# A graph-network stack on one core: the row of f_j by one small transpose and four SBUF-to-SBUF transfers, LayerNorm and mask in place, five groups

## The chip, the cores and the metric

The kernel runs on one core of one Trainium2 chip, as one program. The metric is the device time of that core in microseconds, as the median of several runs. The kernel before takes 2701.74 us (three runs, 2699.85 to 2704.03).

## The reference

128 graphs of 128 nodes with 256 features each go through four layers, all in float32. Each layer is followed by a residual sum and a LayerNorm. The first is a gated graph network of three steps, the other three are graph attention with different weights:

```python
# layer 0, three times:
m = jnp.einsum('bnd,de->bne', h, weight[i])
aggr = jnp.einsum('bst,bsd->btd', A, m)          # A = (adj != 0)
h = _gru_cell(aggr, h, w_ih, w_hh, b_ih, b_hh)
# layers 1 to 3:
Wh = jnp.einsum('bnf,of->bno', h, W)
f_i, f_j = Wh @ a1, Wh @ a2
e = f_i[:, :, None] + f_j[:, None, :]
e = jnp.where(e > 0, e, ALPHA * e)
e = jnp.where(adj == 0, NEG_INF, e)
h_prime = jnp.einsum('bij,bjo->bio', jax.nn.softmax(e, axis=2), Wh)
# after each layer
x = _layernorm(x + layer(x, adj, ...))
```

What the change touches is the second term of `e`: for every graph the vector f_j, one value per node, has to stand as a row in all 128 partitions, because partition i holds row i of the scores.

## The kernel before, in words

The graphs are worked in 32 groups of G = 4. For a group, `gru` (L477) loads x and the adjacency, turns the adjacency into a float mask (L489), transposes x (L369), and runs three steps. A step aggregates the states over the graph (L504) and forms the gates by `strassen` (L434): seven block products for each of two calls, matmuls of 128x128 by 128x256 (L451), accumulated in PSUM banks of the tag `gate`. DVE adds the parts (L456), ACT takes them out (L512, L516, L519), tanh comes from ACT (L530, L559), the mixing of old and new state from DVE and POOL (L546 to L569). After each step the state is transposed back (L585). After the third, x is loaded again into a buffer `y` (L575), the state is added (L588), and the mask is turned into a bias of 0 or a very large negative number (L576).

Then `gat` (L601) runs the three attention layers of the group. The scores' two vectors f_j (h = 1) and f_i (h = 0) come from eight DVE multiplications with a running sum, one for each graph and vector (L611), which land as columns of a small tile `f`. The row of f_j is made on TensorE: four transposes (L620) of a column that is broadcast to 128 columns, one for each graph, into one PSUM bank. DVE adds the bias and takes the row's maximum (L625), ACT applies the leaky slope (L629) and the exponential (L646), TensorE transposes the weights (L653), multiplies them with the features (L669) and with the layer's matrix (L680), DVE adds the residual (L686), and `layernorm` (L375) follows: mean (L391), squares on ACT (L394), 1/sqrt on POOL (L397, L401), scale and shift on ACT (L407). The group's result is stored (L693).

Nothing of this is issued in the order of the source. Each operation is put into `Plan` with the engines that may run it, a duration for each, what it reads and writes, and a priority. `Plan.order` simulates the engines with these durations and emits the instructions in the order in which they started there; on the chip every engine works through its own list in that order. An operation starts only when its operands are due and when slots for its buffers are free:

```python
LATENCY = {"PE": 250, "ACT": 220, "DVE": 200, "POOL": 250, "SP": 4000}
```

is added between a producer and a consumer on another engine (a transfer counts 4000 ns from its issue, and `lag` on top), and a consumer on TensorE gets 500 ns more. Buffers come in tags with a fixed number of slots, among them `k4` (4 KB a partition), `k2` (2 KB), `bank` (3 PSUM banks), `gate` (5 PSUM banks), `v` (small columns), and `gru`, which has no memory and only limits how many groups are in their gated steps at once; `own` keeps a part of the slots for the oldest group. The priority comes from `stage` (L696): group g has the first number g throughout, and the last four groups (LAST = 4) go step by step together. SyncE (SP) issues all bulk transfers, in order. An operation that names `port=BOTH` is not placed beside another[...]; by default only POOL's operations hold it.

## Time and profile before

| | |
|---|---|
| time, median of three runs | 2701.74 us |
| span of the profiled execution | 2698.8 us |
| busy TensorE / DVE / ACT / POOL | 98 / 75 / 65 / 22% |
| DMA moved in all | 65.39 MB, 24 GB/s over the span |

A matmul in float32 of L451 shows up as two records, one of weights and data each, a transpose as one. Records of TensorE overlap[...]. What an instruction takes of the engine is read from start to start. "PEld" is the loading of weights, which runs beside matmuls.

### The profile page before, as it was taken

How to read it: one execution, taken by the hardware profiler on the slowest of the kernel's cores; microseconds unless marked ns; L12 is line 12 of the kernel's file. 1: busy time of each engine (PE TensorE's matmuls, PEld its weight loads, DVE VectorE, ACT ScalarE, POOL GpSimd, SP SyncE). 2: the span in 40 equal slices, each digit the busy share in tenths (PEclk: the TensorE clock that was granted, in tenths of full speed). 3: DMA queues.
4: the chain of work that ended last, by engine and by line, in shares of the span. 5: the costliest groups of instructions: out<-in, count | busy, mean ns of one | idle time of the engine just before them, and what ended most of it. 6: DMA issues, size and time to landing. Idle time of an engine off the chain costs nothing.

```text
span 2698.8 us, 42460 instructions
## 1 busy us (share of the span) xinstructions
PE 2655.6 (98%) x14536; PEld 2366.9 (88%) x14536; DVE 2019.6 (75%) x6195; ACT 1758.2 (65%) x4633; POOL 603.7 (22%) x749
## 2 busy tenths in 40 slices
PE   8999999999999999999999999999999999999997
PEld 7888889898888888888888888988988988888875
DVE  4676777787777787778777777877778776786796
ACT  4565667666667576666666676666666676765478
POOL 1123222222121221222221221211222211322111
PEclk9999999999999999999999999999999999999999
DMA  3100000000000000001010000000000100000000
GB/s 106 32 13 28 28 13 24 28 29 20 16 21 20 28 28 28 28 1 36 21 36 13 20 24 21 28 28 20 17 28 21 36 21 1 24 9 22 19 1 32
DMA packets 70105, 65.39 MB, mean 24 GB/s; under 512 B 2688, under 2 KB 68224, under 8 KB 69888
## 3 DMA queue, kind: packets, MB, share of 16 engines
q1 hardware_dynamic: 69456, 62.66, 7.7%
q8 instruction: 114, 1.87, 0.3%
q14 instruction: 103, 0.84, 0.1%
q10 hardware_dynamic: 432, 0.01, 0.0%
HBM read 45.89 MB, written 16.78 MB: 23 GB/s over the span
## 4 chain that ended last, share of the span: by engine, by line
PE 90%; DVE 6%; ACT 2%; issue 1%; DMA 0%; POOL 0%; POOLq 0%; ACTq 0%; SPq 0%; DVEq 0%
PE gate L451 61%; PE bank L680 10%; PE bank L504 6%; PE bank L669 6%; PE bank L585 3%; PE bank L620 1%; PE bank L653 1%; DVE fx L611 1%; PE bank L369 1%; PE bank L338 1%; DVE k L686 1%; ACT k L407 1%; DVE k L456 1%; DVE k L289 1%; ACT k L394 0%
## 5 line engine op out<-in xcount | busy, mean ns | idle before, releaser
L451 PE MATMUL gate<-k,whs 128*128 128x256 f32 x4032 | 1201.6, 380 | 3.0 <-DVE k L456 1.4
L451 PE MATMUL gate<-k,wcs 128*128 128x256 f32 x4032 | 1199.2, 379 | 0.0
L451 PEld LDWEIGHTS gate<-k,wcs 128*128 128x128 f32 x4032 | 766.1, 190 | 104.0
L451 PEld LDWEIGHTS gate<-k,whs 128*128 128x128 f32 x4032 | 728.5, 190 | 85.3 <-DVE k L456 2.7
L456 DVE TENSOR_TENSOR k<-gate,k 128x512 f32<-128x512 f32 x576 | 390.4, 686 | 242.3 <-PE gate L451 200.2
L287 ACT COPY k<-bank 128x512 f32<-128x512 f32 (+1 forms) x456 | 262.2, 583 | 207.4 <-PE bank L669 60.9
L680 PE MATMUL bank<-gwT,k 128*128 128x256 f32 x1536 | 350.4, 380 | 3.3 <-ACT k L287 1.5
L680 PEld LDWEIGHTS bank<-gwT,k 128*128 128x128 f32 x1536 | 289.7, 190 | 46.0 <-DVE k L289 4.3
L611 DVE SCALAR_TENSOR_TENSOR fx<-k,wa 128x256 f32<-128x256 f32 x768 | 290.3, 436 | 40.3 <-ACT k L407 38.2
L421 POOL TENSOR_TENSOR k<-k,k 128x256 f32<-128x256 f32 x288 | 236.0, 838 | 372.8 <-DVE k L569 103.6
L394 ACT ACTIVATE k<-k,v 128x256 f32<-128x256 f32 x384 | 190.2, 497 | 185.6 <-DVE v L391 185.1
L407 ACT ACTIVATE k<-k,v,v 128x256 f32<-128x256 f32 x512 | 263.6, 591 | 55.9 <-DVE v L403 53.9
L530 ACT ACTIVATE k<-k,brz 128x512 f32<-128x512 f32 (+1 forms) x384 | 226.9, 620 | 93.2 <-DVE k L456 93.1
L686 DVE SCALAR_TENSOR_TENSOR k<-bank,v,k 128x256 f32<-128x256 f32 x384 | 169.9, 480 | 147.0 <-PE bank L680 145.8
L512 ACT COPY k<-gate 128x512 f32<-128x512 f32 x288 | 164.6, 579 | 127.9 <-PE gate L451 127.0
L564 POOL TENSOR_TENSOR k<-k,k 128x512 f32<-128x512 f32 x82 | 108.5, 1324 | 418.0 <-ACT k L559 418.0
L669 PEld LDWEIGHTS bank<-k,k 128*128 128x128 f32 x1536 | 187.1, 193 | 14.6 <-ACT k L287 5.4
L669 PE MATMUL bank<-k,k 128*128 128x128 f32 x1536 | 189.8, 277 | 8.0 <-DVE k L289 4.0
L289 DVE COPY k<-bank 128x512 f32<-128x512 f32 x228 | 154.3, 684 | 56.2 <-PE bank L504 18.3
L559 ACT ACTIVATE k<-k,bi 128x512 f32<-128x512 f32 x192 | 136.8, 720 | 76.3 <-DVE k L556 59.2
L397 POOL TENSOR_SCALAR v<-v 128x4 f32<-128x4 f32 x96 | 21.1, 220 | 739.3 <-ACT k L394 733.3
L421 POOL TENSOR_TENSOR k<-k 128x256 f32<-128x256 f32 x117 | 100.2, 858 | 340.4 <-DVE k L569 118.2
(78 smaller groups left out, 3166.8 us busy)
## 6 DMA issues: line engine op xcount, KB each, us to landing
xs<-in_x_dram SPq DMA_DIRECT2D x32, 512.0 KB, 3.9
k<-in_x_dram SPq DMA_DIRECT2D x32, 512.0 KB, 3.9
out_dram<-k SPq DMA_DIRECT2D x32, 512.0 KB, 2.9
adj<-in_adj_dram SPq DMA_DIRECT2D x32, 256.0 KB, 2.8
k<-in_gnn_wT_dram SPq DMA_DIRECT2D x3, 256.0 KB, 4.8
k<-in_w_ihT_dram SPq DMA_DIRECT2D x2, 384.0 KB, 5.7
k<-in_w_hhT_dram SPq DMA_DIRECT2D x2, 384.0 KB, 5.7
k<-in_gat_w_dram SPq DMA_DIRECT2D x3, 256.0 KB, 5.1
```

What stands on the lines that cost most here:

```text
L287: nc.scalar.copy(dst, src)
L289: nc.vector.tensor_copy(dst, src)
L394: plan.op({"ACT": 490}, lambda e, b=b: nc.scalar.activation(T(dst)[:, b, :], T(y)[:, b, :], AF.Square, bias=T(mean)[:, b:b + 1], accum_out ...
L407: plan.op({"ACT": 500}, lambda e, b=b: nc.scalar.activation(T(dst)[:, b, :], T(y)[:, b, :], AF.Identity, bias=T(shift)[:, b:b + 1], scale= ...
L421: nc.vector if e == "DVE" else nc.gpsimd).tensor_tensor(T(t)[:, j, :], a(), b(), ALU.subtract),
L451: nc.tensor.matmul(T(dst)[:, j * H:(j + 1) * H], T(w)[:, m, gt, :], moving(m, ms)[1](), start=first and n == 0, stop=n == len(todo) - 1, s ...
L456: plan.op({"DVE": 630}, lambda e: nc.vector.tensor_add(T(o)[:, :, j * H:(j + 1) * H], T(b_).rearrange("p (g n) -> p g n", g=2), T(part).re ...
L530: nc.scalar.activation(T(o)[:, gt, n0:n1], src(), AF.Tanh, bias=brz[:, gt * KC + c:gt * KC + c + 1], scale=0.5)
L611: plan.op({"DVE": 345}, lambda e, b=b, h=h, l=l, f=f, fx=fx, xc=xc: nc.vector.scalar_tensor_tensor(T(fx), T(xc)[:, b, :], 1.0, T(wa)[:, l, ...
L669: nc.tensor.matmul(T(b_)[:, b * P:(b + 1) * P], T(xc)[:, b, c * P:(c + 1) * P], T(pT)[:, b, :], start=True, stop=True)
L680: nc.tensor.matmul(T(b_)[:, (b - b0) * D:(b - b0 + 1) * D], T(aT[k])[:, b * P:(b + 1) * P], T(gwT)[:, l, k, :], start=(k == 0), stop=(k == ...
L686: nc.vector.scalar_tensor_tensor(T(y)[:, b, :], T(b_)[:, (b - b0) * D:(b - b0 + 1) * D], T(rden)[:, b:b + 1], T(xc)[:, b, :], op0=ALU.mult ...
```

## The change

The row of f_j takes another way, for all groups but the last four. One transpose turns the 128x4 columns of f_j into a tile of 4x128 in PSUM; ACT or DVE copies it to SBUF (`row`); then SyncE issues four transfers, one for each graph, which read one row of 512 bytes and write it to all 128 partitions of the score tile `e_`. The bias is added to it in place (L625 of before). The purpose is to take work off TensorE and to hold the PSUM bank more briefly.

The other edits change buffers and order. LayerNorm writes into its own input, with the squares into a scratch tile `jx`. The adjacency is loaded into the mask's own buffer, so that the tag `adj` goes. The second load of x starts after the first tanh of the last step and not after the first aggregation. There may be five groups in their gated steps and six masks, `fx` has one slot, the reserves of `own` are other ones, and the attention of group g has the priority g + 1.5.

```diff
-    pools = {"gru": 4, "xs": 2, "adj": 2, "am": 5, "k2": 26, "k4": 19, "fx": 2, "f": 3, "mv": 4, "st": 6, "v": 16,
+    pools = {"gru": 5, "xs": 2, "am": 6, "k2": 26, "k4": 19, "fx": 1, "jx": 1, "f": 3, "row": 3, "mv": 4, "st": 6, "v": 16,
              "gate": 5, "bank": 3}
-    own = ({"k2": 8, "k4": 5, "gate": 2, "v": 5, "fx": 0, "st": 0}, {"k2": 4, "k4": 2, "v": 5, "fx": 0, "st": 0})
+    own = ({"k2": 6, "k4": 5, "v": 5, "fx": 0, "jx": 0, "st": 0}, {"k2": 6, "k4": 3, "v": 5, "fx": 0, "jx": 0, "st": 0})
...
-                plan.op({"ACT": 490}, lambda e, b=b: nc.scalar.activation(
-                    T(dst)[:, b, :], T(y)[:, b, :], AF.Square, bias=T(mean)[:, b:b + 1], accum_out=T(ss)[:, b:b + 1]),
-                    reads=[(y, b), mean], writes=[(dst, b), (ss, b)], prio=prio)
+                jx = Buf("jx", D)
+                plan.op({"ACT": 490}, lambda e, b=b, jx=jx: nc.scalar.activation(
+                    T(jx), T(y)[:, b, :], AF.Square, bias=T(mean)[:, b:b + 1], accum_out=T(ss)[:, b:b + 1]),
+                    reads=[(y, b), mean], writes=[jx, (ss, b)], prio=prio)
...
-                T(dst)[:, b, :], T(y)[:, b, :], AF.Identity, bias=T(shift)[:, b:b + 1], scale=T(rstd)[:, b:b + 1]),
-                reads=[(y, b), shift, rstd], writes=[(dst, b)], prio=prio)
+                T(y)[:, b, :], T(y)[:, b, :], AF.Identity, bias=T(shift)[:, b:b + 1], scale=T(rstd)[:, b:b + 1]),
+                reads=[(y, b), shift, rstd], writes=[(y, b)], prio=prio)
...
-                plan.op({"SP": 60}, lambda e: nc.sync.dma_start(T(y), x_g), reads=[agg[0]], writes=[y], prio=prio)
+                plan.op({"SP": 60}, lambda e: nc.sync.dma_start(T(y), x_g), reads=[(nn[0], 5)], writes=[y], prio=prio)
...
             b_ = bank()
-
-            def fn(e, b_=b_, f=f):
+            if g < NG - LAST:
+                row = Buf("row", P)
+                plan.op({"PE": 150}, lambda e, b_=b_, f=f: nc.tensor.transpose(T(b_)[0:G, 0:P], T(f)[:, :, 1], ident),
+                        reads=[(f, 2 * b + 1) for b in range(G)], writes=[b_], prio=prio)
+                plan.op({"ACT": 250, "DVE": 200}, lambda e, b_=b_, row=row: copy(e, T(row)[0:G, :], T(b_)[0:G, 0:P]),
+                        reads=[b_], writes=[row], prio=prio)
                 for b in range(G):
-                    nc.tensor.transpose(T(b_)[:, b * P:(b + 1) * P],
-                                        T(f)[:, b, 1:2].to_broadcast([P, P]), ident)
-            plan.op({"PE": 440}, fn, reads=[(f, 2 * b + 1) for b in range(G)], writes=[b_], prio=prio)
+                    plan.op({"SP": 330}, lambda e, b=b, row=row, e_=e_: nc.sync.dma_start(
+                        T(e_)[:, b, :], T(row)[b:b + 1, :].unsqueeze(1).to_broadcast([1, P, P])),
+                        reads=[row], writes=[(e_, b)], prio=prio, lag=1500)
+                rows, keys, port = (lambda b, e_=e_: T(e_)[:, b, :]), lambda b: [], BOTH
+            else:
+                def fn(e, b_=b_, f=f):
+                    for b in range(G):
+                        nc.tensor.transpose(T(b_)[:, b * P:(b + 1) * P],
+                                            T(f)[:, b, 1:2].to_broadcast([P, P]), ident)
+                plan.op({"PE": 440}, fn, reads=[(f, 2 * b + 1) for b in range(G)], writes=[b_], prio=prio)
+                rows, keys, port = (lambda b, b_=b_: T(b_)[:, b * P:(b + 1) * P]), lambda b, b_=b_: [b_], ("POOL",)
 
             for b in range(G):
-                plan.op({"DVE": 215}, lambda e, b_=b_, b=b, e_=e_, top=top: nc.vector.tensor_tensor_reduce(
-                    T(e_)[:, b, :], T(b_)[:, b * P:(b + 1) * P], T(no)[:, b, :], 1.0, 3 * FAR, ALU.add, ALU.max,
-                    T(top)[:, b:b + 1]), reads=[b_, no], writes=[(e_, b), (top, b)], prio=prio)
+                plan.op({"DVE": 215}, lambda e, rows=rows, b=b, e_=e_, top=top: nc.vector.tensor_tensor_reduce(
+                    T(e_)[:, b, :], rows(b), T(no)[:, b, :], 1.0, 3 * FAR, ALU.add, ALU.max,
+                    T(top)[:, b:b + 1]), reads=keys(b) + [no, (e_, b)], writes=[(e_, b), (top, b)], prio=prio, port=port)
...
-            xn = Buf("k4", G, D)
-            layernorm(y, total, xn, prio)
-            xc = xn
+            layernorm(y, total, prio)
+            xc = y
...
-        return g if g < tail else tail + n, 2 * g + (n >= STEPS)
+        return g + 1.5 * (n >= STEPS) if g < tail else tail + n, 2 * g + (n >= STEPS)
```

More of the change, by code (lines that the diff above doesn't have):

```diff
@@ L221, in adj_resnorm_kernel @@
     psum = ctx.enter_context(tc.tile_pool(name="psum", bufs=1, space=bass.MemoryType.PSUM))
-    pools = {"gru": 4, "xs": 2, "adj": 2, "am": 5, "k2": 26, "k4": 19, "fx": 2, "f": 3, "mv": 4, "st": 6, "v": 16,
+    pools = {"gru": 5, "xs": 2, "am": 6, "k2": 26, "k4": 19, "fx": 1, "jx": 1, "f": 3, "row": 3, "mv": 4, "st": 6, "v": 16,
              "gate": 5, "bank": 3}
-    own = ({"k2": 8, "k4": 5, "gate": 2, "v": 5, "fx": 0, "st": 0}, {"k2": 4, "k4": 2, "v": 5, "fx": 0, "st": 0})
-    floats = {"gru": 0, "k4": 1024, "xs": 1024, "fx": 256, "f": 8, "mv": 8, "st": 6, "v": 4}
+    own = ({"k2": 6, "k4": 5, "v": 5, "fx": 0, "jx": 0, "st": 0}, {"k2": 6, "k4": 3, "v": 5, "fx": 0, "jx": 0, "st": 0})
+    floats = {"row": 128, "gru": 0, "k4": 1024, "xs": 1024, "fx": 256, "jx": 256, "f": 8, "mv": 8, "st": 6, "v": 4}
     tags = {t: (n, floats.get(t, 512)) for t, n in pools.items()}
@@ L230, in adj_resnorm_kernel @@
     plan = Plan({t: n for t, (n, _) in tags.items()}, own)
-    slots = {t: [(psum if t in ("gate", "bank") else work).tile([P, w], I32 if t == "adj" else F32, name=f"{t}{i}")
+    slots = {t: [(psum if t in ("gate", "bank") else work).tile([P, w], F32, name=f"{t}{i}")
                  for i in range(n)] for t, (n, w) in tags.items() if w}
@@ L373, in transposed, with layernorm @@
         return res
-    def layernorm(y, total, dst, prio):
+    def layernorm(y, total, prio):
         rstd, ve, shift = Buf("v", G), Buf("v", G), Buf("v", G)
@@ L477, in gru @@
     def gru(g, stage):
-        xs, adj_i, am = Buf("xs", G, D), Buf("adj", G, P), Buf("am", G, P)
+        xs, am = Buf("xs", G, D), Buf("am", G, P)
         prio = stage(g, 0)
@@ L483, in gru @@
         plan.op({"SP": 450}, lambda e: nc.sync.dma_start(T(xs), x_g), writes=[xs], prio=prio)
-        plan.op({"SP": 60}, lambda e: nc.sync.dma_start(T(adj_i), adj[g * G:(g + 1) * G].rearrange("b s t -> s b t")),
-                writes=[adj_i], prio=prio)
+        plan.op({"SP": 60}, lambda e: nc.sync.dma_start(T(am).bitcast(I32), adj[g * G:(g + 1) * G].rearrange("b s t -> s b t")),
+                writes=[am], prio=prio)
         if g == 0:
@@ L488, in gru @@
             hidden_weights(prio)
-        plan.op({"DVE": 417}, lambda e: nc.vector.tensor_scalar(T(am), T(adj_i), 0, None, op0=ALU.not_equal),
-                reads=[adj_i], writes=[am, turn], prio=prio, port=BOTH)
+        plan.op({"DVE": 417}, lambda e: nc.vector.tensor_scalar(T(am), T(am).bitcast(I32), 0, None, op0=ALU.not_equal),
+                reads=[am], writes=[am, turn], prio=prio, port=BOTH)
         hT = transposed(xs, lambda b, c: T(xs)[:, b, c * P:(c + 1) * P], prio)
@@ L596, in gru @@
                 h, hT = h2, hT2
-        x1 = Buf("k4", G, D)
-        layernorm(y, None, x1, prio)
-        return x1, am
+        layernorm(y, None, prio)
+        return y, am
     def gat(g, xc, no, stage):
```

## The prediction

> **What bounds the kernel now.** I read the page first (busy shares, then the chain that ended last), then the busy time by stage, then the order in time around one set of the transposes that go.

> The page's busy shares and its chain that ended last:

> ```profile
> PE 2655.6 (98%) x14536; PEld 2366.9 (88%) x14536; DVE 2019.6 (75%) x6195; ACT 1758.2 (65%) x4633; POOL 603.7 (22%) x749
> ...
> PE 90%; DVE 6%; ACT 2%; issue 1%; DMA 0%; POOL 0%; POOLq 0%; ACTq 0%; SPq 0%; DVEq 0%
> PE gate L451 61%; PE bank L680 10%; PE bank L504 6%; PE bank L669 6%; PE bank L585 3%; PE bank L620 1%; PE bank L653 1%; DVE fx L611 1%; PE bank L369 1%; PE bank L338 1%; DVE k L686 1%; ACT k L407 1%; DVE k L456 1%; DVE k L289 1%; ACT k L394 0%
> ```

> TensorE is busy 98% of the span and 90% of the chain is TensorE itself: almost never a wait, nearly always the instruction before. L620, the set of four transposes that the change takes out, is named in it with 1%.

> Busy time of each engine by stage (columns: stretch, length, PE, PEld, DVE, ACT, POOL, granted clock, DMA share and GB/s):

> ```profile
> 0.00:200.00 200.00, 188.28 (x956) 162.41 (x957) 125.37 (x298) 105.59 (x246) 36.24 (x45) 0.99 0.17 51
> 200.00:400.00 200.00, 198.47 (x1088) 177.24 (x1087) 142.18 (x421) 125.77 (x325) 47.22 (x58) 1.00 0.07 22
> 400.00:2400.00 2000.00, 1995.12 (x11029) 1789.82 (x11029) 1531.94 (x4697) 1328.16 (x3513) 471.74 (x584) 1.00 0.08 23
> 2400.00:2600.00 200.00, 199.70 (x1054) 176.61 (x1052) 145.14 (x375) 117.13 (x282) 32.03 (x38) 1.00 0.05 14
> 2600.00:2698.80 98.80, 74.03 (x414) 60.86 (x414) 74.94 (x408) 81.55 (x271) 16.51 (x26) 0.95 0.07 22
> ```

> The average hides two kernels. From 400 to 2400 us TensorE idles 4.9 us in 2000; DVE idles 23% and ACT 34% there. All of TensorE's idle time is 2698.8 - 2655.6 = 43.2 us, of which 11.7 lie in the first 200 us and 24.8 in the last 99. So in the middle a microsecond less of matmul is a microsecond less of span, as long as the others keep feeding TensorE; the end is another matter.

> One set in the order of time of TensorE (start, duration, then the instruction):

> ```profile
> 1003.80 0.59 PE L451 MATMUL gate<-k,wcs 128*128 128x256 f32 x2
> 1004.23 0.60 PE L620 MATMUL bank<-ident,f 128*128 128x128 f32 x4
> 1004.67 0.60 PE L451 MATMUL gate<-k,whs 128*128 128x256 f32 x2
> ```

> Durations overlap; the starts count. The next matmul starts 1004.67 - 1004.23 = 0.44 us after the set does, so one transpose takes 0.11 us of TensorE, though its record says more (next fence). A pair of L451 records takes 0.43 us.

> [...] No transfer of the kernel before reads so few partitions, so the trace is silent; this is the main risk. [...] L546, both inputs in SBUF, averages 743 ns; L456, one input in PSUM, 686.

> **The change part by part.** The rows that price it, from the groups of instructions and the DMA issues (busy, mean ns; for DMA us to landing):

> ```profile
> L620 PE MATMUL bank<-ident,f 128*128 128x128 f32 x384 | 59.1, 274 | 2.5 <-DVE fx L611 1.3 <-DVE k L686 1.0
> L625 DVE CUSTOM_DVE_ANT_0 k<-bank,am 128x128 f32<-128x128 f32 x384 | 88.3, 285 | 12.2 <-PE bank L620 11.8
> L519 ACT COPY k<-gate 128x256 f32<-128x256 f32 x288 | 105.2, 366 | 0.0
> ```

> ```profile
> k<-in_x_dram SPq DMA_DIRECT2D x32, 512.0 KB, 3.9
> adj<-in_adj_dram SPq DMA_DIRECT2D x32, 256.0 KB, 2.8
> ```

> *Removed.* 28 of the 32 groups times 3 layers are 84 sets of four transposes, 84 x 4 x 0.11 = 37.0 us of TensorE; the last four groups keep theirs.

> *Added on TensorE.* 84 small transposes. The identity is still the moving operand with 128 columns, only the stationary side shrinks to four, so I take 0.11 us; the bounds are 0.03 (if four columns cost a quarter) and 0.22 (if its neighbours' weight loads, 190 ns each, were not hidden). 84 x 0.11 = 9.2 us. Net: 37.0 - 9.2 = **27.7 us less**, all of it between 100 and 2600 us, on the path. With the bounds: 34.4 to 18.5.

> *Added copies.* 84 copies of 4x128 from PSUM. The nearest row is L519, 366 ns for twice the columns; I take 0.3 us, 84 x 0.3 = 25 us, on ACT or DVE, hidden in ACT's 34% or DVE's 23% of idle time.

> *Added transfers.* 84 x 4 = 336 of 64 KB each (a row of 512 B, written to 128 partitions), 0.37 us each for SyncE to issue: 124 us in all on a queue with some 130 issues in it, hidden. Landing: 256 KB take 2.8 us and 512 KB 3.9, so 1.1 us per 256 KB and 1.7 fixed; 64 KB come to 2.0 us. The four are issued within 1.1 us, so the last row is there 3.1 us after SyncE starts, or 5 if an x load lies ahead of it. [...] The plan in the code allows 4 x 0.33 + 1.5 + 4.0 = 6.8 us for the last row. I take something at or below 6.8, then DVE finds its rows there.

> *The added wait.* It is L625's, for the transfer. Behind it on DVE, which runs in order, stand the additions L456 that empty the gate banks, and TensorE waits for these. Within the 6.8 us nothing waits, since the order puts other work ahead of L625.

> *DVE.* The reduce reads two SBUF operands in place of PSUM and SBUF. By [...]L546 against L456 at most 8% longer: 336 x 0.02 = 8 us, in DVE's idle time. Its four no longer hold one of the three PSUM banks: a small gain for TensorE, which I don't count.

> *Latency of a layer.* Copy, issue and landing add 4 to 7 us to a layer. Two x loads of L575 start at 988.36 and 1074.23, so a group takes 86 us and a layer's share is 28; the fifth group and the later place of the attention (1.5 later in priority) keep more ready work beside it. In the middle I cost it at nothing: TensorE has other groups' gates to do.

> *In place.* LayerNorm into y, squares into a scratch tile, the mask where its integers landed: the same instructions, cost 0; k4 buffers come free earlier. One slot of fx or jx alters the order alone, since one engine writes it. The y load now starts after the first tanh of the last step; between are three DVE operations of 0.69 us and the transposes of 0.44, 2.5 us, against 3.9 to land, so L588 comes up to 1.4 us later, 32 x 1.4 = 45 us of one of three banks, off TensorE's path.

> *Start and end.* The last four groups keep the old form, and the 24.8 us idle in the last 99 us stay. I leave the first 200 us as they are too.

> Sum: 2701.7 - 27.7 = **2674.0 us**.

> **Rivals.** A, the forecast: transfers within their time, TensorE still dense, 2674; with the bounds 2667 to 2683.

> B, denser too: freed buffers, the shorter hold of a bank and the fifth group also remove the middle's 6.7 us of idle and half of the first 200 us' 11.7: 27.7 + 6.7 + 5.9 = 40.3, 2661. For it: waits for banks are what TensorE's few gaps consist of. Against: there is little left to gain.

> C, gain eaten: the long round trip costs TensorE some 0.25 us in each of the 84 layers, 21 us, so 2695. For it: a static order fits one set of latencies. Against: DVE idles 28 x 0.23 = 6.5 us a layer, which absorbs such slips.

> D, slower: [...] For it: [...]DVE's order. Against: L625 has lower priority than the next group's gates, so often stands later than its rows' due time, and the four rows are wanted one after another.

> **How the numbers follow.** A 0.58, B 0.10, C 0.12, D 0.20. The time is A's. For eight in ten the range takes A with its bounds, B to 2656 and C with a little of D's mild end, to 2714; most of D stays out. The limits of 0.2% are 2696.3 and 2707.1: A, B and half of C are below, 0.74; between lies 0.08 (the rest of C and the edge of D); above 0.18.

> **What would show it.** Right: TensorE busy about 28 us lower with its share still 98%, the middle's idle time still near 5 us in 2000, the row transfers landing in 2 to 6 us, the groups showing 84 small transposes with 0.11 us between their start and the next, and no wait of DVE for a DMA above some tens of us. Wrong: waits of L625 for the transfers of hundreds of us, TensorE then idling before L451 with L456 as the releaser[...]. A tail with more than 30 us idle would show that the order got worse at the end.

## The result, and the profile after

The changed kernel takes 3001.11 us (median of four runs, 2997.41 to 3005.13) beside 2702.81 us of the kernel before: 1.1106 times as long, 95% interval 1.1086 to 1.1125. It is 298 us slower where 27.7 us less were forecast.

The page of the changed kernel, busy shares and the chain that ended last. Its lines are shifted: L452 is L451 of before, L457 is L456, L638 is the reduce (L625 of before), L620 the small transpose, and L625 is now the transfer of a row.

```profile
PE 2755.8 (92%) x14284; PEld 2400.4 (80%) x14284; DVE 2091.3 (70%) x6220; ACT 1770.2 (59%) x4600; POOL 706.0 (24%) x841
...
PE 53%; DMA 22%; DVE 15%; ACT 5%; issue 3%; SPq 2%; POOL 1%; POOLq 0%; ACTq 0%; DVEq 0%
PE gate L452 31%; DMA k<-row 21%; PE bank L693 8%; PE bank L682 5%; PE bank L505 4%; DVE k L457 3%; DVE fx L611 2%; DVE k L289 2%; PE bank L586 2%; SPq L625 2%; ACT k L659 2%; DVE k L547 1%; PE bank L666 1%; POOL v L402 1%; DVE st L382 1%
```

TensorE fell from 90 to 53% of the chain, and the transfers of the rows, absent before, are 21% of it. TensorE is busy longer in all than before, though it has 252 instructions less.

The stages (stretch, length, PE, PEld, DVE, ACT, POOL, granted clock, DMA share and GB/s):

```profile
200.00:400.00 200.00, 175.47 (x930) 154.15 (x929) 130.22 (x395) 113.60 (x296) 38.03 (x47) 0.95 0.28 27
400.00:2400.00 2000.00, 1849.24 (x9581) 1614.29 (x9580) 1420.96 (x4181) 1180.49 (x3075) 516.88 (x607) 0.95 0.30 29
2900.00:2998.80 98.80, 74.11 (x424) 63.07 (x422) 72.42 (x391) 83.57 (x270) 16.19 (x26) 0.90 0.07 22
```

The loss lies in the middle: TensorE has 9581 records in these 2000 us where it had 11029, idles 150.8 us where it idled 4.9, and its granted clock is 0.95 where it was 1.00. The last 99 us are as before (74.1 us busy, 74.0 before). The DMA engines are busy 30% of the time where they were 8, for 29 GB/s in place of 23: a lot of time for few bytes.

From the groups of instructions and the DMA issues, the rows that answer to those of before:

```profile
L620 PE MATMUL bank<-ident,f 128*4 128x128 f32 x84 | 23.0, 274 | 4.3 <-DVE fx L611 4.0 <-ACT k L513 0.2
L638 DVE CUSTOM_DVE_ANT_0 k<-k,am 128x128 f32<-128x128 f32 x336 | 114.1, 349 | 307.3 <-DMA k<-row 307.3
```

```profile
k<-row SPq DMA_DIRECT2D x336, 64.0 KB, 8.5
xs<-in_x_dram SPq DMA_DIRECT2D x32, 512.0 KB, 4.1
```

The 84 small transposes are there. A row of 64 KB takes 8.5 us to land, twice as long as x with 512 KB. DVE stands 307 us before L638 for it.

How that reaches TensorE is seen in one place: first SyncE, which issues the transfers, then DVE, then TensorE, each in order of time:

```profile
1256.34 16.83 SPq L625 DMA_DIRECT2D k<-row  x8
```

```profile
1263.62 0.29 DVE L638 CUSTOM_DVE_ANT_0 k<-k,am 128x128 f32<-128x128 f32 x1 [1.66 <-DMA k<-row]
...
1266.17 0.29 DVE L638 CUSTOM_DVE_ANT_0 k<-k,am 128x128 f32<-128x128 f32 x1 [1.90 <-DMA k<-row]
1266.39 0.08 DVE L638 DVE_READ_ACCUMULATOR2_ANT v<- 128x1 f32 x1
1268.22 0.29 DVE L638 CUSTOM_DVE_ANT_0 k<-k,am 128x128 f32<-128x128 f32 x1 [1.75 <-DMA k<-row]
1268.44 0.08 DVE L638 DVE_READ_ACCUMULATOR2_ANT v<- 128x1 f32 x1
1268.44 0.69 DVE L457 TENSOR_TENSOR k<-gate,k 128x512 f32<-128x512 f32 x1
```

```profile
1265.82 0.59 PE L452 MATMUL gate<-k,wcs 128*128 128x256 f32 x2
1271.60 1.22 PE L452 MATMUL gate<-k,whs 128*128 128x256 f32 x2 [5.18 <-DVE k L457]
1272.61 1.06 PE L452 MATMUL gate<-k,wcs 128*128 128x256 f32 x2
```

The line of SyncE spans the issues of two layers, four transfers each, with a pause of 8.8 us between them. The four of the first layer start at 1256.34 to 1258.14 and land at 1260.91, 1263.60, 1266.15 and 1268.20. DVE finds the first row there and waits 1.7 to 1.9 us before each of the other three. So it goes in 54 of the 84 layers; in 19 DVE does not wait at all. The gate additions L457 stand behind; TensorE uses up what it has and waits 5.18 us for them. Then its matmuls start 1.01 us apart where they started 0.43 apart. The windows of 4 us over this place say why (the column before the last two is the granted clock):

```profile
1262.00:1266.00 4.00, 4.00 (x22) 3.54 (x21) 0.65 (x4) 1.00 (x3) 0.00 (x0) 1.00 0.72 25
1266.00:1270.00 4.00, 0.41 (x2) 0.01 (x1) 2.08 (x10) 1.32 (x4) 0.00 (x0) 0.97 0.28 11
1270.00:1274.00 4.00, 2.40 (x7) 1.94 (x8) 3.61 (x11) 3.51 (x12) 0.80 (x1) 0.50 0.68 25
1274.00:1278.00 4.00, 4.00 (x19) 3.75 (x18) 3.44 (x6) 0.77 (x2) 1.50 (x2) 0.68 0.72 25
```

The granted clock falls to 0.50 in the idle stretch, 3.3 us after its start, and stays there for 6.8 us, the last 5.0 of them after TensorE has begun again. The 300.0 us between the two spans add up: idle 43.2 before and 243.0 after, so 199.8 more; busy 2655.6 before and 2755.8 after, so 100.2 more, although about 27.7 us of work went. That leaves 127.9 us of longer work, most of it the lower clock: the trace has the clock at 0.50 for 259.9 us, TensorE is busy in 190.1 of them, and at half the rate 95 are lost; before it was 3. So the clock costs about 92 us, an estimate. The other 36 stay open. TensorE stops more often, with 210 busy stretches where it had 59, and the last record of each has no next one to overlap with; that may be it, but no run shows it alone.

### The profile page after: what moved, and what is told of

Same layout as the page of the kernel before. It is cut to its first block, busy times and chain, and to the rows that moved or that the text cites. A ratio compares the mean times of both kernels' runs of the same rounds, so it can differ in the third digit from the quotient of the medians.

```text
span 2998.8 us, 42377 instructions
## 1 busy us (share of the span) xinstructions
PE 2755.8 (92%) x14284; PEld 2400.4 (80%) x14284; DVE 2091.3 (70%) x6220; ACT 1770.2 (59%) x4600; POOL 706.0 (24%) x841
## 4 chain that ended last, share of the span: by engine, by line
PE 53%; DMA 22%; DVE 15%; ACT 5%; issue 3%; SPq 2%; POOL 1%; POOLq 0%; ACTq 0%; DVEq 0%
PE gate L452 31%; DMA k<-row 21%; PE bank L693 8%; PE bank L682 5%; PE bank L505 4%; DVE k L457 3%; DVE fx L611 2%; DVE k L289 2%; PE bank L586 2%; SPq L625 2%; ACT k L659 2%; DVE k L547 1%; PE bank L666 1%; POOL v L402 1%; DVE st L382 1%
## 5 line engine op out<-in xcount | busy, mean ns | idle before, releaser
L452 PE MATMUL gate<-k,whs 128*128 128x256 f32 x4032 | 1242.8, 391 | 124.5 <-DVE k L457 106.9
L452 PE MATMUL gate<-k,wcs 128*128 128x256 f32 x4032 | 1225.0, 386 | 0.0
L452 PEld LDWEIGHTS gate<-k,whs 128*128 128x128 f32 x4032 | 743.3, 195 | 238.6 <-DVE k L457 125.5
L452 PEld LDWEIGHTS gate<-k,wcs 128*128 128x128 f32 x4032 | 785.2, 195 | 113.1
L457 DVE TENSOR_TENSOR k<-gate,k 128x512 f32<-128x512 f32 x576 | 390.7, 686 | 287.0 <-PE gate L452 205.9
L565 POOL TENSOR_TENSOR k<-k,k 128x512 f32<-128x512 f32 x134 | 171.7, 1282 | 1306.7 <-ACT k L560 1303.7
L642 ACT ACTIVATE k<-k,f 128x128 f32<-128x128 f32 x384 | 148.3, 400 | 375.9 <-DVE v L638 375.8
L611 DVE SCALAR_TENSOR_TENSOR fx<-k,wa 128x256 f32<-128x256 f32 x768 | 343.7, 448 | 14.0 <-ACT k L408 3.6
L638 DVE CUSTOM_DVE_ANT_0 k<-k,am 128x128 f32<-128x128 f32 x336 | 114.1, 349 | 307.3 <-DMA k<-row 307.3
L422 POOL TENSOR_TENSOR k<-k,k 128x256 f32<-128x256 f32 x344 | 273.5, 809 | 230.0 <-ACT k L287 65.3
L531 ACT ACTIVATE k<-k,brz 128x256 f32<-128x256 f32 (+1 forms) x384 | 233.8, 623 | 75.6 <-DVE k L457 75.6
L395 ACT ACTIVATE jx<-k,v 128x256 f32<-128x256 f32 x384 | 193.8, 505 | 114.2 <-DVE v L391 108.1
L289 DVE COPY k<-bank 128x512 f32<-128x512 f32 x293 | 198.0, 685 | 87.3 <-PE bank L666 30.2
L659 ACT ACTIVATE k<-k,v 128x128 f32<-128x128 f32 x384 | 149.4, 390 | 43.0 <-DVE v L655 40.6
## 6 DMA issues: line engine op xcount, KB each, us to landing
xs<-in_x_dram SPq DMA_DIRECT2D x32, 512.0 KB, 4.1
k<-in_x_dram SPq DMA_DIRECT2D x32, 512.0 KB, 4.2
out_dram<-k SPq DMA_DIRECT2D x32, 512.0 KB, 3.2
am<-in_adj_dram SPq DMA_DIRECT2D x32, 256.0 KB, 2.8
k<-in_gnn_wT_dram SPq DMA_DIRECT2D x3, 256.0 KB, 5.6
```

The costliest lines, as they stand in the source:

```text
L289: nc.vector.tensor_copy(dst, src)
L395: plan.op({"ACT": 490}, lambda e, b=b, jx=jx: nc.scalar.activation(T(jx), T(y)[:, b, :], AF.Square, bias=T(mean)[:, b:b + 1], accum_out=T( ...
L422: nc.vector if e == "DVE" else nc.gpsimd).tensor_tensor(T(t)[:, j, :], a(), b(), ALU.subtract),
L452: nc.tensor.matmul(T(dst)[:, j * H:(j + 1) * H], T(w)[:, m, gt, :], moving(m, ms)[1](), start=first and n == 0, stop=n == len(todo) - 1, s ...
L457: plan.op({"DVE": 630}, lambda e: nc.vector.tensor_add(T(o)[:, :, j * H:(j + 1) * H], T(b_).rearrange("p (g n) -> p g n", g=2), T(part).re ...
L531: nc.scalar.activation(T(o)[:, gt, n0:n1], src(), AF.Tanh, bias=brz[:, gt * KC + c:gt * KC + c + 1], scale=0.5)
```

## Experiments: is it where the rows lie?

The theory, T: the transfers are slow because of where their rows lie, each in one partition and the four in partitions 0 to 3; DVE stands before them and starves TensorE. The rivals: S, small transfers are slow whatever they read; O, the new order and the buffers cost the time; L, five groups cannot hide a longer layer.

**Reading 128 partitions.** The same transfers in the same order, from another place:

```diff
-  nc.tensor.transpose(T(b_)[0:G, 0:P], T(f)[:, :, 1], ident)
+  nc.tensor.transpose(T(b_)[:, 0:P], T(f)[:, 0, 1:2].to_broadcast([P, P]), ident)
...
-  T(e_)[:, b, :], T(row)[b:b + 1, :].unsqueeze(1).to_broadcast([1, P, P])
+  T(e_)[:, b, :], T(row)
```

> The changed kernel with the same 336 transfers of 64 KB in 128 packets of 512 bytes, in the same order, but each reads 128 partitions in place of one: the small transpose makes the row of the first graph in all 128 partitions, and each transfer copies it partition by partition. It leaves out the rows of f_j of the other three graphs. Theory T: the packets take 30 to 60 ns in place of about 220, landing falls from 8.5 to between 2 and 3 us, the wait of DVE for the transfers from 307 to below 30 us, and the time is 2665 to 2690 us. Rival S (small transfers, their issue or their number are slow in themselves): landing stays above 6 us and the time above 2900. Rival O: landing falls but the time stays above 2800.

It took 2672.24 us, 0.9892 times the kernel before (0.9877 to 0.9907). Packets of 512 bytes, those of the rows and of the adjacency together, took 27 ns in the median, where those of the changed kernel took 220. The page's busy shares, the middle stage and the landing:

```profile
PE 2630.0 (98%) x14284; PEld 2341.2 (88%) x14284; DVE 2083.2 (78%) x6220; ACT 1747.9 (65%) x4600; POOL 698.7 (26%) x841
```

```profile
400.00:2400.00 2000.00, 1998.83 (x10954) 1788.14 (x10954) 1605.98 (x4750) 1330.06 (x3520) 573.61 (x685) 1.00 0.11 33
```

```profile
k<-row SPq DMA_DIRECT2D x336, 64.0 KB, 1.9
```

Same number, size and order of transfers; landing 1.9 in place of 8.5 us, no wait of DVE for rows in the waits, the clock at 1.00 in the middle, 329 us gone. S and O fall as the main cause.

**Four rows 36 partitions apart.** A kernel in which DVE first spreads the columns of f_j to 4x32, so that the transpose gives 32 copies of each row, was run with two sources for the transfers. In the first of them each transfer reads one partition, and the four are 0, 36, 72 and 108:

```diff
-  T(row)[b:b + 1, :].unsqueeze(1).to_broadcast([1, P, P])
+  T(row)[36 * b:36 * b + 1, :].unsqueeze(1).to_broadcast([1, P, P])
```

> As the run with the spread source, but each transfer reads one partition again: partition 36 b for graph b[...]. If the DMA engines take the transfers strictly one after another[...]: landing near 4.6, 7.3, 9.8 and 11.9 us after the first issue, 2950 to 3060 us. If the engines overlap transfers, the four go in parallel: all landed within some 6 us, below 2800 us.

Counted from the first issue of a layer, the medians over its 84 layers and those of the changed kernel are:

| row | changed kernel, us | 36 apart, us | 128 partitions, us |
|---|---|---|---|
| 1 | 4.59 | 4.01 | 1.81 |
| 2 | 7.28 | 4.85 | 2.46 |
| 3 | 9.83 | 5.34 | 3.09 |
| 4 | 11.88 | 6.90 | 3.73 |

The rows land as in the second answer of the expectation, though the last at 6.9 us and not at 6: with the rows 36 partitions apart they follow one another by 0.5 to 1.6 us. In the changed kernel, from partitions 0 to 3, they do so by 2.05 to 2.7 us: 65,536 bytes in 2.43 us on average, 27.0 GB/s. What makes the one set of partitions slower than the other is not shown. The time was still 2953.43 us (1.0932, 1.091 to 1.0953), as in the first answer, and most of that is not the rows: the next run has the same order.

**32 partitions a transfer**, all of f_j computed:

```diff
+  nc.vector.tensor_copy(T(fw).rearrange("p (b r) -> p b r", b=G), T(f)[:, :, 1:2].to_broadcast([P, G, 32]))
-  nc.tensor.transpose(T(b_)[0:G, 0:P], T(f)[:, :, 1], ident)
+  nc.tensor.transpose(T(b_)[:, 0:P], T(fw), ident)
...
-  T(row)[b:b + 1, :].unsqueeze(1).to_broadcast([1, P, P])
+  T(row)[32 * b:32 * b + 32, :].unsqueeze(1).to_broadcast([32, G, P])
```

> The changed kernel, computing all it should, with the rows' source spread: DVE copies each column of f_j 32 times into a tile of 128x128 (one more instruction for a group's layer, two row slots in place of three for space), the one transpose then yields 32 copies of each graph's row, and a transfer reads 32 partitions four times each in place of one 128 times. [...] packets of 30 to 60 ns, landing 1.8 to 3 us, DVE's wait for rows below 30 us, 2662 to 2690 us, so faster than both kernels. If reading a partition more than once is what is slow[...], landing stays above 4 us and the time above 2750.

The rows landed within 2.09 to 4.03 us, as expected. The time, 2919.22 us (1.0802, 1.0786 to 1.0818), is 34 us below the run with rows 36 partitions apart but 229 us above the expected range. TensorE waits elsewhere (waits of TensorE, total, times, longest):

```profile
PE bank L669 <- ACT k L662: 59.3, 16, 5.9
PE bank L623 <- DVE fw L620: 39.8, 11, 9.3
```

The additional copy and the softmax come late in this order. I had taken two row slots in place of three for space. With three, and one slot for the spread tile:

> The run with the spread source of 32 partitions again (2919 us, rows landed by 4.0 us, TensorE waiting up to 9 us for the spread copy), with three row slots as in the changed kernel and one unreserved slot for the spread tile, in place of two and two. If the two row slots made that order bad (a slot is held until the planned landing, and one is kept for the oldest group): 2665 to 2700 us. If the spread source or the additional DVE copy is what costs: above 2800 us.

2743.11 us (1.0156, 1.0139 to 1.0173), between the two answers. The 2919 us lie 244 above the best version found below (2675). Of these, 176 go with the two slot counts, which were not tried apart; the other 68 stay open, since the copy and its one slot change the order too.

## Experiments: latency, order and the other edits

**The measured due times given to the plan**, the transfers as slow as ever:

```diff
-  reads=[row], writes=[(e_, b)], prio=prio, lag=1500)
+  reads=[row], writes=[(e_, b)], prio=prio, lag=(1500, 3300, 5500, 7300)[b])
```

> The changed kernel, with one edit: the plan's lag of the four row transfers is 1.5, 3.3, 5.5 and 7.3 us in place of 1.5 for all, so that the order expects the rows at 5.8, 8.0, 10.5 and 12.6 us after the first issue; the trace shows 4.6, 7.3, 9.8 and 11.9. The transfers themselves stay as slow. Theory T in its weak form (what costs is that DVE meets the wait, not the latency): DVE's wait below 60 us, the clock back at 0.99 or more, 2670 to 2720 us. Rival L (five groups cannot hide a longer layer): 2850 us or more with little wait of DVE for transfers, and TensorE idle for lack of ready work.

2735.33 us (1.0127, 1.0111 to 1.0142): 266 us of the loss are gone without a faster transfer. The waits of this kernel:

```profile
DVE k L638 <- DMA k<-row: 66.1, 52, 7.4
...
PE bank L369 <- DMA xs<-in_x_dram: 29.5, 6, 12.1
```

DVE waits 66 us for rows in place of 307, just over what was expected, and the time is 15 us above the expected range. The latency of 12 us is nearly hidden once the order knows it; L falls. What remains includes 29.5 us of TensorE waiting for x, where it is 19.5 in the changed kernel and 7.2 in the best version below.

**The row's way alone**, on the kernel before (one slot of fx, two of the row, for space):

> The kernel before with only the row's new way: small transpose, copy, four transfers; LayerNorm not in place, adjacency in its own buffer, four groups, old priorities (fx with one slot and two row slots, for space). Theory T: as slow as the changed kernel or slower, since one group less stands ready, 2990 to 3150 us, with DVE waiting 300 us or more for the rows. Rival O: near 2700 us.

3101.45 us (1.1482, 1.1457 to 1.1507). DVE waited 404 us for rows. So the other edits do not cause the loss. The changed kernel is 100 us faster, but this run has two row slots where it has three, and slots alone were worth up to 176 us above; what the other edits save beside slow rows is not shown.

**The other edits alone**, with the four old transposes in every group:

```diff
-  if g < NG - LAST:
+  if False:
```

> All other edits of the change (LayerNorm and mask in place, five groups, the later priority of the attention, the later load of x), but the row of f_j by the four old transposes in every group. Theory T (the transfers are slow[...], DVE stands before them and TensorE starves): no transfer, so no loss, 2690 to 2712 us, TensorE busy near 2655 us and the clock at 0.998. Rival O (the new order and the buffers cost the time, whatever the row's way): 2850 us or more.

2731.12 us (1.0111, 1.0094 to 1.0127): 30 us slower, which I had not expected. TensorE idles 65.3 us in its profile where it idled 43.2. Four runs look for the reason, the first with these lines of the kernel before:

```diff
-  own = ({"k2": 6, "k4": 5, "v": 5, ...
+  own = ({"k2": 8, "k4": 5, "gate": 2, "v": 5, ...
-  "gru": 5 ... "fx": 1
+  "gru": 4 ... "fx": 2
-  return g + 1.5 * (n >= STEPS) if g < tail ...
+  return g if g < tail ...
```

> The kernel with old transposes and only the edits of buffers: LayerNorm in place with the scratch tile, the adjacency in the mask's buffer with six masks, the later load of x; four groups, the old reserves, the old priorities, two slots of fx. It splits the 30 us that the other edits cost together. If the order (fifth group, priority, reserves) costs them: 2690 to 2710 us. If the buffers or the later load do: 2718 us or more.

2702.44 us (1.0004, 0.9995 to 1.0013). Buffers in place and the later load of x cost nothing, as forecast; the 30 us go with what sets the order: the groups, the reserves, the priority and the slot of fx.

> The run of the other edits with old transposes (2731 us) with two slots of fx, as before, in place of one. If the one slot, which makes the order place the eight multiplications further apart, costs the 30 us: 2697 to 2712 us. If the groups, reserves and priority do: 2720 us or more.

2717.74 us (1.0059, 1.0042 to 1.0076): between the two answers. The one slot of fx accounts for about 13 of the 30 us.

> The same run of the other edits (2731 us) with four groups in place of five. If the fifth group costs the 30 us: 2697 to 2712 us. If the priority and the reserves do: 2720 us or more; less than the two together may come out, since each of these runs has another order.

2741.71 us (1.015, 1.0135 to 1.0165): without the fifth group it gets slower, so that is not it.

```diff
+  plan.op(EVICT, lambda e, b_=b_, e_=e_: copy(e, T(e_).rearrange("p b j -> p (b j)"), T(b_)), ...)
-  rows, keys, port = (lambda b, b_=b_: T(b_)[:, b * P:(b + 1) * P]), lambda b, b_=b_: [b_], ("POOL",)
+  rows, keys, port = (lambda b, e_=e_: T(e_)[:, b, :]), lambda b: [], BOTH
```

> The run of the other edits with old transposes in every group (2731 us, 30 above the kernel before), with one edit: for the first 28 groups the four transposed rows are copied from PSUM to the score tile at once, by ACT or DVE, and the bias is added there, so that the PSUM bank is not held until four additions of low priority are done. If the held bank is what costs the 30 us: 2690 to 2708 us. If the new order costs them otherwise: 2720 us or more.

2726.68 us (1.0092, 1.0077 to 1.0108). The held bank is worth about 4 us, with the copies paid. What the rest of the 30 us is (priority or reserves) was not tried apart.

## Experiments: does the forecast gain exist?

**Rows four partitions apart in the changed kernel's own order.** The tile of the two vectors gets four columns a graph, so that the transpose puts the rows of f_j into partitions 1, 5, 9 and 13, at no further instruction in the loop:

```diff
-  f = Buf("f", G, 2)
+  f = Buf("f", G, 4)
-  nc.tensor.transpose(T(b_)[0:G, 0:P], T(f)[:, :, 1], ident)
+  nc.tensor.transpose(T(b_)[0:4 * G, 0:P], T(f).rearrange("p b c -> p (b c)"), ident)
...
-  T(row)[b:b + 1, :].unsqueeze(1).to_broadcast([1, P, P])
+  T(row)[4 * b + 1:4 * b + 2, :].unsqueeze(1).to_broadcast([1, P, P])
```

> The changed kernel, computing all it should, in the same order and with the same slots; only the tile f has four columns a graph in place of two, so that the small transpose puts the rows of f_j into partitions 1, 5, 9 and 13 in place of 0 to 3. [...] the transfers then overlap: landing near 4.0, 4.8, 5.3 and 6.9 us after the first issue, where the order expects 5.8 to 6.8. Theory T[...]: DVE's wait for rows below 40 us, 2665 to 2690 us, faster than both kernels. Rival (the run with the spread source was slow at 2919 us although its rows landed within 4.0 us[...]): above 2800 us.

2687.34 us (0.9947, 0.9933 to 0.9962), faster than both kernels. Rows land 3.86, 4.72, 5.17 and 6.66 us after the first issue, which is what the order expects. It misses the other run's 2672 by 15 us, and the groups of instructions name a wait:

```profile
L623 PE MATMUL bank<-ident,f 128*16 128x128 f32 x84 | 23.0, 274 | 15.3 <-DVE fx L614 14.9 <-DVE k L292 0.4
```

The small transpose reads the whole tile, f_i too, so on the chip it also waits for the four later multiplications, of which the plan knows nothing.

**f_j in a tile of its own:**

```diff
-  f = Buf("f", G, 4)
+  f, fj = Buf("f", G, 2), Buf("fj", G, 4)
-  accum_out=T(f)[:, b, h:h + 1]
+  accum_out=T(fj if h else f)[:, b, 0:1]
```

> The run[...] again (2687 us), with f_j in a tile of its own. In that run the small transpose read the whole tile with f_i in it, so on the chip it waited for the four later multiplications too, which the order does not allow for: TensorE and its weight loads sat before it 38 us. With the tiles apart that wait goes: 2666 to 2680 us, TensorE idle near 41 us, as in the run that read 128 partitions. If the longer landing[...] is what costs the 15 us between the two: 2684 to 2692 us.

2674.62 us (0.9899, 0.9885 to 0.9914), 27.6 us below the 2702.27 us of the kernel before beside it. The busy shares, the middle stage and the small transpose:

```profile
PE 2631.1 (98%) x14284; PEld 2340.3 (88%) x14284; DVE 2083.7 (78%) x6223; ACT 1747.6 (65%) x4600; POOL 701.0 (26%) x841
```

```profile
400.00:2400.00 2000.00, 1999.14 (x10951) 1786.20 (x10950) 1606.66 (x4754) 1329.73 (x3519) 574.50 (x684) 1.00 0.20 33
```

```profile
L623 PE MATMUL bank<-ident,fj 128*16 128x128 f32 x84 | 22.9, 273 | 0.6 <-DVE k L292 0.4 <-ACT k L516 0.2
```

The wait before the transpose fell from 15.3 to 0.6 us, TensorE idles 0.9 us in the middle 2000, and a landing of 4.1 us in the median is as good as one of 1.9. This is the best version found, faster than the kernel before and 327 us faster than the changed one.

**The last four groups too:**

```diff
-  if g < NG - LAST:
+  if True:
```

> The same with the new way of the row in the last four groups too. Another 12 sets of transposes go, 12 x 0.33 = 4.0 us of TensorE, but in the last 100 us TensorE waits anyway and a layer there gets the round trip of 4 to 7 us three times: 2672 to 2700 us, slower than its neighbour by 5 to 20 us.

2691.09 us (0.9962, 0.9947 to 0.9977), 16 us slower than its neighbour. From 2400 us to the end TensorE is busy 244 us in both and idle 44 in place of 29: too little other work is left at the end to fill the round trip, it seems.

**The old order with rows four partitions apart.** The whole edit of buffers and the row's way as in the run with four columns a graph, but four groups, the old reserves and priorities:

> [...] with the edits of buffers and the row's way, but four groups, the old reserves and the old priorities. If the gain does not need the new order: 2665 to 2690 us. If the fifth group and the later priority are needed to hide the round trip: 2700 us or more.

2707.59 us (1.0024, 1.0017 to 1.0031), 20 us above that run in the new order. The kernel before with only the row's way, from 32 partitions a transfer:

> The kernel before with only the row's new way, with the source spread over 32 partitions a graph as in the run beside it (one slot each for the row and the spread tile, fx with one, for space); LayerNorm, mask, groups and priorities as before. If the gain of the removed transposes does not hang on the other edits: 2662 to 2690 us. If the longer round trip needs the fifth group and the later priority to be hidden: 2700 us or more, with TensorE's idle time well above 43 us.

2712.35 us (1.004, 1.0025 to 1.0055), with 70.7 us of idle TensorE; its single slots share the doubt of the other runs with the spread tile. The first of the two, beside the run with four columns a graph in the new order, is the cleaner one: only groups, reserves and priority differ. The wait for rows, in the old order and then in the new:

```profile
DVE k L641 <- DMA k<-row: 41.5, 60, 1.8
```

```profile
DVE k L641 <- DMA k<-row: 1.5, 5, 0.5
```

So 20 us of the gain hang on the fifth group, the reserves and the later priority together, which help to hide the round trip. Which of the three does it is not shown.

## Why the prediction was wrong, step by step

*The failed step* is the landing under "Added transfers". I had 3.1 us from the size and the 6.8 us that the plan allows, and took "something at or below 6.8, then DVE finds its rows there", for which nothing in the trace spoke, since no transfer in it reads so few partitions. The last row lands 11.9 us after the first issue, 5.1 after the order's due time, and moving the rows to other partitions brings 3.7 (128 partitions a transfer) or 6.6 (rows four partitions apart). With that the added wait, put at nothing, became 307.3 us of DVE. The trace before could not decide it, and the slower outcome, rival D, was given a chance of 0.20 and mostly left out of the range.

*Rival D had the direction*: rows later than the plan allows, DVE standing before them, TensorE short of work. How much later was the author's estimate, and the trace did not show it. Measured are 307.3 us of DVE before L638, 3.7 us a layer, and 3001.1 - 2674.6 = 326.5 us above the kernel in which only the rows' partitions and the tile of f_j differ. Of DVE's 307 us some 200 reach TensorE as idle time, so about 107 were absorbed, 1.3 us a layer, less than one product of 4 x 0.43 = 1.7 us. And D lacked a term: about 92 us, by the estimate above, are TensorE's lower clock.

*Removed and added on TensorE* was right. The small transpose's neighbour starts 146.17 - 146.06 = 0.11 us after it in the order of time of TensorE, as assumed, and with rows four partitions apart the time is 2674.6 us against 2674.0 forecast. That is another kernel than the one that was changed, and an agreement to 0.6 us is in part luck: TensorE's busy time fell by 24.5 us and not by 27.7, and the order, put at nothing, is worth 20 us beside fast rows.

*Issue by SyncE*, 0.37 us each and "hidden": wrong in size. It is 0.59 us in the median of the changed kernel and up to 2.5. The first three of a layer take 0.47 to 0.59 us in the median in every version; the fourth takes 2.23 in the changed kernel, 1.4 to 1.5 with rows 4 or 36 partitions apart and 0.6 with 32 or 128 partitions a transfer. So it goes with the pace of the transfers before it; how is not shown. In the place shown the fourth starts 1.8 us after the first, not 1.1.

*Added copies, reads of SBUF by the reduce*: right in kind. L638 takes 349 ns where L625 took 285, 22% more and not 8 (medians 292 and 285, the longest 1264 and 293). The 8% compared means, and the medians of L546 and L456 are 685 and 688 ns, so the trace before did not price this. 336 x 0.064 = 21.5 us on DVE, hidden in the run with f_j's own tile, where DVE is busy 78%.

*In place at nothing*: right (2702.4 beside 2701.8). *Latency of a layer and the later place at nothing*: right only beside the rows' new way. With the old transposes that order, with its one slot of fx, costs 30 us, with fast rows it saves 20. The plan's order fits one set of latencies, as rival C said, but I looked for it in the wrong edit.

*Start and end*: right; TensorE is busy 189.3 us of the first 200 (188.3 before) and 74.1 of the last 99 (74.0).

## What to carry to other kernels

Four transfers that each repeat one partition were priced here by which partitions these are, not by their size: 11.9 us for all four from partitions 0 to 3, 6.6 to 6.9 from partitions 4 or 36 apart. So try what is to be broadcast from several rows in partitions further apart, which here cost nothing but the columns' place. In a kernel with an order written ahead, a latency that the order knows costs little (12 us known: 34 us over the 2701 beside it, 61 over the best version; the same 12 us taken for 6.8: 298), so measure the landing and enter it before judging the idea. And look at what a wait delays after it ends: beside 200 us of idle time about 92 more, by the estimate above, came from the clock.
